# Four small moves in the preparation stage of a four-layer sequence kernel: gate DMAs on ScalarE, modulations in earlier gaps, a QR mask on GpSimd, a division ahead of a QR piece

## The chip, the cores and the metric

The kernel runs on one core of a Trainium2 chip. The metric is the device time of one execution in microseconds (us); of several executions the median is taken. The engines are named as the profile names them: PE is TensorE (matmuls), PEld its weight loads, DVE is VectorE, ACT is ScalarE, POOL is GpSimd, SP is SyncE, which issues most DMAs. A "q" behind a name (SPq, ACTq) is the engine's sequencer, issuing a DMA or taking a branch.

## The reference, cut to what matters

The input `x` is 32 sequences of 128 tokens and 144 channels; `cond` is one vector of 144 per sequence. Four layers follow each other:

- L0: a transformer block. A modulation vector of 6 x 144 per sequence comes from `swish(cond) @ w_mod + b_mod`: a shift and a scale for attention and MLP each, and two gates. Layernorm, modulate, attention with 16 heads of 9 (queries and keys layernormed), gated residual; layernorm, modulate, MLP with GELU, gated residual.
- L1: `U = qr(P).Q` of a 144 x 64 matrix; a 64 x 64 skew matrix per sequence is built from `cond`, `R = expm(A)`; then `x + (z R - z) U^T` with `z = x U`.
- L2: a block like L0 without the norm of queries and keys, with modulations of its own.
- L3: attention as in L2 and a mixture of four experts (two per token), with modulations of its own.

```
mod = swish(c) @ w_mod + b_mod            # once for L0, L2 and L3
U, _ = jnp.linalg.qr(P);  R = expm(A(cond))
x_rot = x + einsum('btd,nd->btn', z @ R - z, U)
```

## The kernel before, in words

All of `x` stays in SBUF. The kernel walks through **ticks**, from -6 to the end; in each tick one sequence of a layer is at each station of a software pipeline. The station "scores" works on the sequence of this tick (`s0`, its row maxima) and of the tick before (`s1`, its exponentials), "weigh", "sums", "divide" and "project_out" on that of two ticks before (`s2`). Layer 0's 32 sequences start at ticks 0 to 31, layer 1's (L2) at tick 39 (`first`, L1163). Nothing reorders the program: each engine executes its instructions in the order in which the Python code emits them. That order is written by hand: in a tick (L1289 to L1325) the named gaps "a", "e", "t", "stats", "b0", "b", "den", "pre1", "c", "y1", "y2", "d", "z" stand between the stations, and `put` (L1168) hangs other work into (tick, gap).

Beside layer 0 two preparations run, both Python generators of which a gap executes one piece.

- `prep_qr` (L313) makes the Householder QR of `P`, 64 columns, three pieces each. The first broadcasts column j by two PE matmuls (L324), takes two sums of squares on ACT (`n2` L334, `ss` L337) and a copy (L336), and a root on POOL (`nrm`, L335). The second is on DVE: a dot product (L340, waits for ACT), the signed root (L345, waits for POOL), three small steps (L349 to L351), and the mask `m` (L352, from `ss`). The third, on DVE too, makes the weight `w` (L354, L355, which uses `m`) and updates the matrix (L356), which the next column's L324 needs. `prepare_qr` (L1129) places one column in each tick before 0, and two in each tick from 0 to 28: pieces one to three in gaps "a" and "t", and then "den", "y1" and "y2".
- `prep_expm` (L420) first makes the modulations and gates of L2 and L3 (`modulations(1)`, `modulations(2)`, each with `layer_gates`), then the skew matrices from eight loaded parts W4 (four loaded at the start, four issued behind the first use, L448), then the matrix exponentials. `prepare_expm` (L1152) executes one piece at (-2, "z"), and from tick 0 on one at "b" and one at "z".

`layer_gates` (L280) makes the two gate vectors of a layer on PE, copies them to one SBUF buffer `gsb` on ACT (L291; the buffer has one copy, so the next call's copy waits for the DMAs out of it), and SP sends them to DRAM in two DMAs (L293), from where they are later broadcast. The weights of the last modulation (L134, into `mlps`) are loaded in `first_gates` at (-4, "b"), issued by SP behind the gate DMAs.

DMA completion is counted on eight semaphores that all queues share in turn; the issuing engine waits until the previous DMA on the same semaphore has landed.

At the end of a tick of layer 0, `divide_T` (L901, PE) spreads the reciprocal sums into PSUM, gap "y1" follows (a second QR piece on DVE), then `divide` (L906, DVE, multiplies the weighted values into `oT`), gap "y2" (a third QR piece), "d", and after "z" `project_out` (L927, PE), which reads `oT`; `residual` (L916) follows on DVE and L913 on POOL.

Of the kernel before, what the change touches and what calls it, by code (L numbers as in the profile page):

```python
# [12 lines left out]
ALU = mybir.AluOpType  # L13
# [40 lines left out]
TINY = 1e-18  # L54
# [11 lines left out]
def tile_kernel(ctx: ExitStack, tc: tile.TileContext, a: dict, out: bass.AP):  # L66
    nc = tc.nc
# [212 lines left out]
    def layer_gates(n):  # L280
        w = w_mods[n]
        psg = bank([B, 2, C], f"ps_gate{n}")
        for c in range(2):
            for k in range(2):
                rows = slice(0, KH + k)
                nc.tensor.matmul(
                    psg[:, c, :], csT[rows, k, :], w[k][rows, MODC + c * C : MODC + (c + 1) * C],
                    start=k == 0, stop=k == 1,
                )
        gsb = pp.tile([B, 2 * C], F32, tag="gsb", name=f"gsb{n}")  # L290
        nc.scalar.copy(gsb, psg.rearrange("b n c -> b (n c)"))  # L291
        for c in range(2):
            nc.sync.dma_start(  # L293
                gates[n, c].rearrange("(b c) -> b c", c=C), gsb[:, c * C : (c + 1) * C]
            )

# [16 lines left out]
    def prep_qr():  # L313


        u0 = pq.tile([128, D], F32, name="u0")
        ssa = pq.tile([128, D], F32, name="ssa")
        rca = pq.tile([128, D], F32, name="rca")
        tau = pq.tile([128, D], F32, name="tau")
        tri = cst[:, K_TRI : K_TRI + D]  # L320
        for j in range(D):
            n = C - j
            ps = bank([128, n + 1], f"ps_qr{j}")
            nc.tensor.matmul(  # L324
                ps, ident[:, j : j + 1].to_broadcast([128, 128]), at[:, j:], start=True, stop=True
            )
            row = small.tile([128, C + 1], F32, tag="qrr", name=f"qrr{j}", bufs=2)
            s = small.tile([128, 8], F32, tag="qr", name=f"qr{j}")
            d, al, n2, nrm, m, den, w = (s[:, i : i + 1] for i in range(7))
            ss, rec, uj = (t[:, j : j + 1] for t in (ssa, rca, u0))  # L330
            junk = small.tile([128, C], F32, tag="qrj", name=f"qrj{j}", bufs=2)
            junk2 = small.tile([128, C + 1], F32, tag="qrk", name=f"qrk{j}", bufs=1)

            nc.scalar.activation(junk2[:, : n + 1], ps, AF.Square, accum_out=n2)  # L334
            nc.gpsimd.tensor_tensor(nrm, n2, half, ALU.pow)  # L335
            nc.scalar.copy(row[:, : n + 1], ps)  # L336
            nc.scalar.activation(junk2[:, :n], ps[:, 1:], AF.Square, accum_out=ss)  # L337
            yield

            nc.vector.scalar_tensor_tensor(  # L340
                junk[:, : n - 1], at[:, j + 1 : C], 1.0, row[:, 1:n], ALU.mult, ALU.mult,
                accum_out=d,
            )

            nc.vector.scalar_tensor_tensor(  # L345
                al.bitcast(U32), row[:, 0:1].bitcast(U32), 0x80000000, nrm.bitcast(U32),
                ALU.bitwise_and, ALU.bitwise_or,
            )
            nc.vector.tensor_tensor(uj, row[:, 0:1], al, ALU.add)  # L349
            nc.vector.tensor_tensor(den, uj, al, ALU.mult)  # L350
            nc.vector.reciprocal(rec, den)  # L351
            nc.vector.tensor_scalar(m, ss, 4 * TINY * TINY, tri[:, j : j + 1], ALU.is_gt, ALU.mult)  # L352
            yield
            nc.vector.tensor_scalar(w, at[:, j : j + 1], uj, d, ALU.mult, ALU.add)  # L354
            nc.vector.tensor_scalar(w, w, rec, m, ALU.mult, ALU.mult)  # L355
            nc.vector.scalar_tensor_tensor(  # L356
                at[:, j + 1 : C], row[:, 1:n], w, at[:, j + 1 : C], ALU.mult, ALU.add
            )
            yield
        nc.vector.scalar_tensor_tensor(tau, ssa, 4 * TINY * TINY, rca, ALU.is_gt, ALU.mult)  # L360

        idd = ident[:D, :D]
        v = pq.tile([D, C], F32, name="v")
        nc.vector.tensor_tensor(v, at[:D, :C], cst[:D, K_SU : K_SU + C], ALU.mult)
        dg = pq.tile([D, 2, D], F32, name="dg")
        nc.vector.tensor_tensor(dg[:, 0, :], u0[:D], idd, ALU.mult)
        nc.vector.tensor_tensor(dg[:, 1, :], tau[:D], idd, ALU.mult)
        nc.vector.tensor_tensor(v[:, :D], v[:, :D], dg[:, 0, :], ALU.add)
        tc_ = pq.tile([D, 1], F32, name="tauc")
        nc.vector.tensor_reduce(tc_, dg[:, 1, :], AX.X, ALU.add)  # L370
        yield
        ps = bank([KH, 2, D], "ps_vt")
        for k in range(2):
            nc.tensor.transpose(ps[:, k, :], v[:, k * KH : (k + 1) * KH], idd)
        vt = pq.tile([KH, 2, D], F32, name="vt")
        nc.scalar.copy(vt, ps)
        yield
        ps = bank([D, D], "ps_vv")
        for k in range(2):
            nc.tensor.matmul(ps, vt[:, k, :], vt[:, k, :], start=k == 0, stop=k == 1)  # L380
        ml = pq.tile([D, 6, D], F32, name="ml")
        nc.vector.tensor_scalar(ml[:, 0, :], ps, tc_, None, ALU.mult)
        lev = cst[:D, K_LEV : K_LEV + 6 * D].rearrange("p (l c) -> p l c", c=D)
        for i in range(5, -1, -1):
            nc.vector.tensor_tensor(ml[:, i, :], ml[:, 0, :], lev[:, i, :], ALU.mult)
        xs = pq.tile([D, 2, D], F32, name="xs")
        nc.vector.tensor_copy(xs[:, 0, :], idd)
        nc.vector.tensor_copy(xs[:, 1, :], idd)
        yield
        yt = pq.tile([D, D], F32, name="yt")  # L390
        for i in range(6):
            ps = bank([D, D], f"ps_yt{i}")
            nc.tensor.matmul(ps, ml[:, i, :], xs[:, 1, :], start=True, stop=True)
            nc.vector.tensor_copy(yt, ps)
            yield
            ps = bank([D, 2, D], f"ps_z{i}")
            nc.tensor.matmul(ps[:, 0, :], yt, xs[:, 0, :], start=True, stop=True)
            nc.tensor.matmul(ps[:, 1, :], xs[:, 0, :], yt, start=True, stop=True)
            nc.vector.tensor_tensor(xs, xs, ps, ALU.subtract)
            yield  # L400
        ps = bank([D, C], "ps_y")
        nc.tensor.matmul(ps, xs[:, 0, :], v, start=True, stop=True)
        y = pq.tile([D, C], F32, name="y")
        nc.vector.tensor_scalar(y, ps, tc_, None, ALU.mult)
        yield
        ps = bank([128, C], "ps_uT")
        for h in range(2):
            nc.tensor.matmul(ps[h * D : (h + 1) * D], v[:, :D], y, start=True, stop=True)
        nc.vector.tensor_tensor(uT, cst[:, K_I2 : K_I2 + C], ps, ALU.subtract)
        ur = pq.tile([D, 128], F32, name="ur")  # L410
        nc.vector.memset(ur, 0.0)
        nc.vector.tensor_copy(ur[:, :CR], uT[:D, CM:])
        yield
        ps = bank([128, 2, D], "ps_u")
        nc.tensor.transpose(ps[:, 0, :], uT[:D, :CM], idd)
        nc.tensor.transpose(ps[:, 1, :], ur, idd)
        nc.vector.tensor_copy(uM, ps[:, 0, :])
        nc.vector.tensor_copy(uR, ps[:, 1, :])
# [484 lines left out]
    def divide(s):  # L903
        po = st[s]["ot"][:, : 2 * T].rearrange("p (t q) -> p t q", t=2)
        oT = work.tile([128, 2, T], F32, tag="oT", name=f"oT_{s}")
        nc.vector.tensor_tensor(oT, st[s].pop("on"), po, ALU.mult)  # L906
        st[s]["oT"] = oT
# [243 lines left out]

    def prepare_expm(tick, gap):  # L1152
        nonlocal prep_expm
        if prep_expm and (tick >= 0 and gap in ("b", "z") or (tick, gap) == (-2, "z")):
            said = next(prep_expm, 0)
            if said == 0:
                prep_expm = None
            elif said is not None:
                rot_T.append(said)
# [108 lines left out]
    def fill(tick, gap):  # L1268
        prepare_qr(tick, gap)
        while (tick, gap) == (last_prep, "d") and late is None:  # L1270
            prepare_qr(tick, gap)
            prepare_expm(tick, gap)

        if gap == ("t" if tick < 0 else "den" if tick < first[1] else "stats") and tick in stats:
            ln_stats(stats.pop(tick))
        for f, args in gaps.pop((tick, gap), ()):
            f(*args)
        prepare_expm(tick, gap)

    last_prep = first[1] - 8  # L1280
    for tick in range(-6, first[2] + B + 14):
# [24 lines left out]
        joined = tick >= first[1]  # L1306
        if s2 is not None:
            divide_T(s2)
        fill(tick, "y1")
        if s2 is not None and not joined:  # L1310
            divide(s2)
        fill(tick, "y2")
        if not joined:
            fill(tick, "d")
# [178 lines left out]
```

## Time and profile before

| what | value |
|---|---|
| median of 3 runs | 1423.7 us (1420.84 to 1427.12) |
| the profiled execution | 1412.95 us |
| its span (first to last instruction) | 1411.1 us |
| PE busy | 1333.3 us, 94% |
| DVE busy | 798.3 us, 57% |
| ACT busy | 819.2 us, 58% |
| POOL busy | 623.4 us, 44% |
| `ps_qr` matmul of tick -1, 0, 1, 3, 18, 24 starts at | 30.87, 39.44, 51.42, 73.25, 256.37, 346.45 us |

All times of the profile are counted from the start of the span. A tick is found in the PE timeline by its first L324 matmul (gap "a"); layer 0 fills about the first 460 us. In a row of a timeline the columns are start, length, engine, line, operation, output<-inputs, shape, and in brackets the idle time before it with what ended it. In a table of stretches each engine has its busy time and its number of instructions, and PEclk is the share of TensorE's full clock that was granted. The line numbers are those of the kernel before.

### The profile page before, as it was taken

The page shows a single profiled execution, that of the slowest core. Times are in us where ns is not written, and L with a number is a line of the kernel's source. Part 1 is how long each engine was busy: PE and PEld are TensorE (multiplying, and loading weights), DVE is VectorE, ACT ScalarE, POOL GpSimd, SP SyncE. Part 2 cuts the span into 40 slices and gives each one's busy share as a digit, 9 for nine tenths or more (in the row PEclk, how much of TensorE's full clock was granted, in tenths as well). Part 3 has the DMA queues.
Part 4 walks back from the last instruction along what each step waited for, and adds up shares of the span by engine and source line. Part 5 has one row for each costly group of instructions (what it writes and reads, how often), then busy time and mean ns, then how long its engine had stood idle before and what let it go on. Part 6 is the DMA issues. An engine that isn't in the chain of part 4 may idle for free.

```text
span 1411.1 us, 36544 instructions
## 1 busy us (share of the span) xinstructions
PE 1333.3 (94%) x14530; PEld 976.5 (69%) x14530; DVE 798.3 (57%) x2652; ACT 819.2 (58%) x1912; POOL 623.4 (44%) x1647
## 2 busy tenths in 40 slices
PE   6989898999989988999999999999999999999998
PEld 4667576686766566677767666777776767677765
DVE  5798888877864256565555555544444444343211
ACT  3657767656756445666666666555555555554431
POOL 5567667654643433343333334425252525151522
PEclk9999999999999999999999999999999999999999
DMA  8200000000003100000100000200000000000000
GB/s 221 57 2 19 19 19 2 19 3 20 19 1 117 34 2 18 10 19 10 42 27 18 10 18 11 73 10 18 9 19 9 19 10 18 10 18 2 18 9 9
DMA packets 21612, 34.78 MB, mean 25 GB/s; under 512 B 2176, under 2 KB 12256, under 8 KB 21184
## 3 DMA queue, kind: packets, MB, share of 16 engines
q1 hardware_dynamic: 20848, 31.82, 7.7%
q8 instruction: 117, 1.92, 0.6%
q10 hardware_dynamic: 592, 0.59, 0.2%
q14 instruction: 55, 0.45, 0.1%
HBM read 29.93 MB, written 2.47 MB: 23 GB/s over the span
## 4 chain that ended last, share of the span: by engine, by line
PE 68%; DVE 4%; ACT 2%; issue 1%; POOL 1%; POOLq 0%; DVEq 0%
PE ps_h L673 17%; PE ps_f L953 16%; PE ps_s L849 6%; PE ps_w L849 6%; PE ps_qk L673 5%; PE ps_o L876 5%; PE ps_pj L927 3%; PE ps_v L673 2%; PE ps_o L889 1%; DVE nm L854 1%; PE ps_o L901 1%; PE ps_g L673 1%; DVE oT L906 1%; PE ps_z L985 1%; PE ps_o L808 0%
## 5 line engine op out<-in xcount | busy, mean ns | idle before, releaser
L861 ACT ACTIVATE pr<-ps_w 128x512 f32<-128x512 f32 x384 | 208.5, 596 | 165.4 <-PE ps_w L849 164.7
L854 DVE TENSOR_REDUCE nm<-ps_s 128x4 f32<-128x512 f32 x384 | 246.8, 684 | 82.3 <-PE ps_w L849 68.9
L849 PE MATMUL ps_w<-q,kT 32*128 32x128 f32 x3072 | 236.4, 284 | 0.9 <-ACT hR_m L663 0.6
L849 PE MATMUL ps_s<-kT,qT 32*128 32x256 f32 x1536 | 234.8, 408 | 0.1
L849 PEld LDWEIGHTS ps_w<-q,kT 32*128 32x128 f32 x3072 | 198.6, 187 | 16.1 <-issue 3.6
L947 ACT ACTIVATE hid<-ps_h 128x512 f32<-128x512 f32 (+1 forms) x224 | 119.2, 590 | 119.1 <-PE ps_h L673 119.1
L953 PE MATMUL ps_f<-mlps,hid 128*128 128x144 f32 x1280 | 181.2, 292 | 0.5 <-ACT hid L947 0.5
L953 PEld LDWEIGHTS ps_f<-mlps,hid 128*128 128x128 f32 x1280 | 165.1, 191 | 18.4 <-issue 11.6
L913 POOL TENSOR_TENSOR x_sb<-x_sb,res_a 128x144 f32<-128x144 f32 x96 | 47.0, 489 | 266.8 <-DVE res_a L916 266.7
L1064 DVE SCALAR_TENSOR_TENSOR acc<-ps_f,cw,acc 128x144 f32<-128x144 f32 x128 | 46.9, 367 | 197.6 <-PE ps_f L953 175.8
L849 PEld LDWEIGHTS ps_s<-kT,qT 32*128 32x128 f32 x1536 | 135.0, 186 | 26.8 <-issue 9.2
L673 PE MATMUL ps_h<-hM_m,mlps 128*128 128x512 f32 x304 | 143.8, 606 | 0.0
L876 PE MATMUL ps_o<-pr,vaug 128*32 128x128 f32 x3072 | 104.8, 277 | 0.4 <-issue 0.4
L876 PEld LDWEIGHTS ps_o<-pr,vaug 128*32 128x32 f32 x3072 | 78.7, 110 | 33.8 <-PE ps_w L849 19.0
L673 PEld LDWEIGHTS ps_h<-hM_m,mlps 128*128 128x128 f32 x304 | 53.4, 190 | 66.2 <-issue 64.7
L906 DVE TENSOR_TENSOR oT<-on,ps_o 128x256 f32<-128x256 f32 x96 | 40.0, 417 | 96.3 <-PE ps_o L808 92.9
L953 PEld LDWEIGHTS ps_f<-pair,hid 128*128 128x128 f32 x640 | 82.3, 190 | 9.6 <-issue 8.4
L953 PE MATMUL ps_f<-pair,hid 128*128 128x144 f32 x640 | 86.8, 287 | 0.2 <-ACT hid L947 0.2
L913 POOL TENSOR_TENSOR x_sb<-x_sb,res_m 128x144 f32<-128x144 f32 x64 | 32.8, 512 | 111.4 <-DVE res_m L916 111.2
L634 POOL TENSOR_SCALAR rs_m_a<-mv_m_a 128x2 f32<-128x2 f32 x81 | 15.5, 191 | 142.9 <-DVE mv_m_a L632 115.5
L663 ACT ACTIVATE hM_m<-ps_hT_m,modM 128x128 f32<-128x128 f32 x96 | 44.1, 460 | 58.4 <-PE ps_hT_m L661 58.2
L861 ACT ACT_TABLE_LOAD x55 | 70.6, 1283 | 8.4 <-PE ps_w L849 7.6
(312 smaller groups left out, 2823.2 us busy)
## 6 DMA issues: line engine op xcount, KB each, us to landing
gates<-gates SPq DMA_DIRECT2D x48, 288.0 KB, 3.6
x_sb<-in_x SPq DMA_DIRECT2D x8, 288.0 KB, 10.2
out_x<-x_sb SPq DMA_DIRECT2D x8, 288.0 KB, 2.4
mlps<-in_L_mlp SPq DMA_DIRECT2D x2, 1000.0 KB, 6.3
wt<-in_W SPq DMA_DIRECT2D x6, 320.0 KB, 8.0
pair<-in_L_mlp SPq DMA_DIRECT2D x1, 1872.0 KB, 10.1
mlps<-in_L_mlp SPq DMA_DIRECT2D x1, 1872.0 KB, 7.6
mlps<-in_L_wmod SPq DMA_DIRECT2D x4, 290.0 KB, 6.3
```

Source lines behind the costliest of these rows:

```text
L663: nc.scalar.activation(gr[g][f"{k}_{kind}"][:, i, :], ps[:, k == "hR", :], AF.Identity, bias=m[:, sh, b : b + 1], scale=m[:, sc, b : b + 1],)
L673: nc.tensor.matmul(ps, x, y, start=k == 0, stop=k == 1)
L849: nc.tensor.matmul(o, x, y, start=True, stop=True)
L854: nc.vector.tensor_reduce(nmv[:, at0 : at0 + 2, ONE : ONE + 2], view.rearrange("p (r t k) -> p r t k", t=2, k=T), AX.X, ALU.max, negate=True,)
L861: nc.scalar.activation(pr[:, 4 * e : 4 * e + 4, :].rearrange("p s q -> p (s q)"), view, AF.Exp, scale=SCALE,)
L876: nc.tensor.matmul(po[rows4(j), t, :], v[:, 4 * j + 2 * t + r, :], prs[j // 2][:, 4 * (j % 2) + 2 * r + t, :], start=r == 0, stop=r == 1,)
L906: nc.vector.tensor_tensor(oT, st[s].pop("on"), po, ALU.mult)
L913: nc.gpsimd.tensor_tensor(x_sb[:, b, :], x_sb[:, b, :], t, ALU.add)
L927: nc.tensor.matmul(ps, oT[:, t, :], w[:, t, :], start=t == 0, stop=t == 1)
L947: nc.scalar.activation(hid[:n, i], ps[:n], AF.Gelu_apprx_tanh)
L953: nc.tensor.matmul(ps, hid[:, at0, i, :], w2[:, m, :], start=m == 0, stop=m == NFC - 1)
L1064: nc.vector.scalar_tensor_tensor(acc, ps, w, acc, ALU.mult, ALU.add)
```

## The change

The two DMAs of each `layer_gates` are issued by ACT instead of SP. The piece with `modulations(2)` runs at (-1, "b") instead of (0, "b"), so that every later piece of `prep_expm` comes one slot (half a tick) sooner. The mask `m` is computed by POOL in a column's first piece, behind `nrm`, instead of by DVE in the second. In layer 0, `divide` is emitted before gap "y1" instead of after it.

```diff
@@ layer_gates
-            nc.sync.dma_start(
+            nc.scalar.dma_start(
                 gates[n, c].rearrange("(b c) -> b c", c=C), gsb[:, c * C : (c + 1) * C]
             )
@@ prep_qr, first piece
             nc.scalar.activation(junk2[:, :n], ps[:, 1:], AF.Square, accum_out=ss)
+            nc.gpsimd.tensor_scalar(m, ss, 4 * TINY * TINY, tri[:, j : j + 1], ALU.is_gt, ALU.mult)
             yield
@@ prep_qr, second piece
             nc.vector.reciprocal(rec, den)
-            nc.vector.tensor_scalar(m, ss, 4 * TINY * TINY, tri[:, j : j + 1], ALU.is_gt, ALU.mult)
             yield
@@ prepare_expm
-        if prep_expm and (tick >= 0 and gap in ("b", "z") or (tick, gap) == (-2, "z")):
+        if prep_expm and (tick >= 0 and gap in ("b", "z") or (tick, gap) in ((-2, "z"), (-1, "b"))):
@@ the loop over ticks
             divide_T(s2)
-        fill(tick, "y1")
         if s2 is not None and not joined:
             divide(s2)
+        fill(tick, "y1")
         fill(tick, "y2")
```

## The prediction, made before the changed kernel ran

> **What bounds the kernel now.** I read the busy slices of the page first, for where PE is not full, since a PE that is full to the end leaves these edits nothing to win.
>
> ```profile
> PE   6989898999989988999999999999999999999998
> ...
> DVE  5798888877864256565555555544444444343211
> ```
>
> PE is below 9 tenths only in the first third, where the two preparations run beside layer 0, and there DVE stands at 8. The change acts in that part alone. Next the table of stretches, cut at ticks.
>
> ```profile
> 30.87:39.44 8.57, 4.07 (x14) 3.12 (x13) 4.11 (x22) 2.97 (x11) 3.87 (x11) 0.50 0.17 51
> 39.44:51.42 11.98, 11.98 (x144) 8.43 (x143) 8.45 (x36) 5.59 (x22) 6.25 (x20) 0.93 0.02 4
> ...
> 73.25:256.37 183.12, 162.77 (x2115) 126.20 (x2116) 165.18 (x594) 128.21 (x404) 128.26 (x352) 0.98 0.04 12
> ```
>
> The columns are length, busy time of PE, PEld, DVE, ACT and POOL, then the clock. Tick -1 (first row) leaves PE idle for 4.5 of its 8.57 us, at half clock; tick 0 fills PE to the last; ticks 3 to 17 (third row) leave PE 20 us idle in 183. Who ends those waits I took from the list of waits of ticks 3 to 17:
>
> ```profile
> PE ps_qr L324 <- DVE at L356: 6.9, 11, 2.1
> PE ps_o L901 <- DVE rdx L894: 5.7, 7, 1.4
> PE ps_pj L927 <- DVE oT L906: 4.3, 6, 1.0
> ...
> DVE qr L345 <- POOL qr L335: 4.3, 13, 0.4
> DVE qrj L340 <- ACT qrr L336: 1.7, 5, 0.4
> ```
>
> PE waits for DVE; all waits of DVE listed there come to 8.8 us in 183. So **ticks 3 to 17 are DVE's**, ticks -1 and 0 PE's, and ticks 18 to 23 mostly PE's.
>
> **Gate DMAs and modulations (ticks -4 to 1).** They share one stretch and are summed together.
>
> ```profile
> 31.71 0.42 PE L661 MATMUL ps_hT_a<-cst,xr 128*128 128x128 f32 x1
> 36.64 0.87 PE L779 MATMUL ps_qkT<-cst,qkn 128*128 128x128 f32 x3 [4.50 <-DVE qky L750]
> ```
>
> ```profile
> 32.98 0.39 ACT L291 COPY gsb<-ps_gate 32x288 f32<-32x288 f32 x1 [4.68 <-DMA gates<-gsb]
> ```
>
> The first copy into `gsb` ends at 19.52, but SP issues its DMAs only at 24.84, behind five loads of `x_sb`; they land at 32.88, and until then the second copy holds ACT. ACT would issue them at about 19.6: 0.4 to 0.6 us each by the five ACTq issues at the start, inside ACT's idle 1.0 us before 20.56. The second copy then follows its gates at about 31.1 and, behind it, two new issues (1.0 us) stand ahead of the column's L334: at 32.6 instead of 33.28. The queries of L767 come 0.7 us sooner. That would be the whole gain, if PE stayed free.
>
> PE does not stay free, since 80 + 8 matmuls of `modulations(2)` now stand ahead of L779. They need the weights that SP issues at 26.94 and 27.41 and that land at 33.12 and 33.80. SP gets to them about 2 us earlier, but the DMA engines are full until 31 (share 1.1 in every stretch from 20 to 30), with the same bytes ahead of them: I keep 33.8. How long they take is a matter of the clock. At full clock (42.88 to 46.44) it was 3.5 us, at half clock (`modulations(0)`: 11.29 to 15.84, gates 16.96 to 19.09) 6.7 us.
>
> ```profile
> 27.40:30.80 3.40, 3.40 (x89) 3.13 (x87) 2.85 (x15) 0.71 (x2) 0.98 (x3) 1.00 1.10 265
> 30.80:34.20 3.40, 1.33 (x6) 0.86 (x4) 1.97 (x11) 1.22 (x7) 0.69 (x2) 0.50 0.12 28
> ```
>
> The first stretch is `modulations(1)`: PE busy throughout, yet the clock falls to 0.50 right after it and stays there until 41.05. These narrow matmuls do not seem to hold the clock up, so I take half clock: 33.8 + 6.7 = 40.5 for L779 instead of 36.64, **+3.9**; tick 0 loses 3.5 at full clock, **-3.5**; the half clock then lasts a stretch longer, to 44.46, so 3.96 us of other work run at half clock (40.5 to 44.46) instead of 4.41 (36.64 to 41.05), half of the difference, **-0.2**. Sum +0.2. The later W4 loads are used one tick after their issue as now (last landing 9.1 us after the first use ends; PE waited 0.8), with a tick 0 some 2 us shorter against a use at the same gap: I add **+0.3**. Upper bound +2. Lower bound, full clock throughout: 33.8 + 3.5 = 37.3, +0.7 - 3.5, and 4.41 us of half clock saved at half their length, 2.2: -5.0.
>
> The Trainium skill ("TensorE: Matmul & The Clock Gate", What's actually happening) says that about 3.4 us of sustained matmuls release the full clock and an idle window of that length takes it away. By it, filling the gap would keep the clock up and this part would give the -5.0; the stretch of 27.40, busy and followed by 0.50, speaks against it.
>
> The one-slot shift moves no work in or out: what DVE and PE do sooner in each tick they do not do in tick 24. The branch of L594, which stalls PE 2.1 us at 343.8, moves from "z" to "b" of tick 23. Nothing, +-1.5.
>
> **Mask on POOL.** The row of a second column (tick 8) and its neighbours:
>
> ```profile
> 138.87 0.16 DVE L351 RECIPROCAL rca<-qr 128x1 f32<-128x1 f32 x1
> 138.96 0.20 DVE L352 TENSOR_SCALAR qr<-ssa,cst 128x1 f32<-128x1 f32 x1
> 139.07 0.41 DVE L906 TENSOR_TENSOR oT<-on,ps_o 128x256 f32<-128x256 f32 x1
> 139.39 0.27 DVE L354 TENSOR_SCALAR qr<-at,u,qr 128x1 f32<-128x1 f32 x1
> 139.70 0.27 DVE L355 TENSOR_SCALAR qr<-qr,rca 128x1 f32<-128x1 f32 x1
> ```
>
> The group's mean is 195 ns, but from its start to the next one's is 0.11 us: that is what goes. L355 gains a wait on POOL beside its wait on DVE. What a second wait costs is seen at L356: in first columns, where the built program gives it two (DVE and PE), it starts 0.38 us after L355, in second columns with one, 0.31. So 0.111 - 0.075 = 0.036 us a column, over the 34 columns of DVE's ticks (3 to 17, 24, 25): **-1.2**. Bounds: 64 x 0.111 = -7.1 if the wait is free, +1 if POOL's extra 0.28 us each (start of L634 to that of L635) reaches L345. The mask itself is in time: it would end 0.78 us or more ahead of L355 in every column, by the end of `nrm` plus 0.3. L913 and the Newton steps queue behind it, with 1 to 4 us of POOL idle per tick.
>
> The Trainium skill ("VectorE: DVE Perf Modes", The DRAIN you can't avoid) measures semaphores between Vector instructions at no extra cost. By it the step would be -7.1 over all columns; L356's 0.38 against 0.31 differs, and I go by that.
>
> **Division ahead of "y1".** L906 now stands ahead of L340 and waits for L901 on PE. What it should end is PE's wait for `oT`:
>
> ```profile
> 138.30 0.38 PE L901 MATMUL ps_o<-cst,rdx 128*128 128x128 f32 x2
> ...
> 139.53 0.76 PE L927 MATMUL ps_pj<-L_wproj,oT 128*128 128x144 f32 x4 [0.74 <-DVE oT L906]
> 140.62 0.45 PE L324 MATMUL ps_qr<-at,cst 128*128 128x121 f32 x2 [0.34 <-DVE at L356]
> ```
>
> `oT` comes 1 us sooner, but the next thing on PE is L324, and that starts 0.14 us after the end of L356, in 12 of the 15 ticks: the 4.3 us of waits move from L927 to L324. L356 itself is not sooner, as DVE does the same work before it. Where DVE's row maxima end before L901 does, DVE now stands idle with the whole QR column behind it, and L324, ACT and POOL behind that. From the timelines (end of L901 minus end of the second L854): tick 5 107.18 - 106.68, 8 138.68 - 138.18, 10 164.31 - 163.82, 14 215.55 - 215.05, 26 379.87 - 379.37: 0.5 each; tick 13 0.24; the rest of DVE's ticks have 0.2 to 0.7 to spare. **+2.7**. Bounds: -4.3 (all of L927's waits) and +4.5 (0.5 in all nine ticks with a shortfall, 18, 27 and 28 being the others).
>
> **Sum.** +0.2 + 0.3 - 1.2 + 2.7 = **+2.0 us**. The profiled execution took 1412.95 (span 1411.1 and 1.85 around it), 10.75 below the median of the three runs; it becomes 1415.0. On the scale of the median, 1423.7 + 2.0 = **1425.7**.
>
> **Rivals.** *Faster*: the clock stays up in tick -1 (-5.0) and the second wait is free (34 x 0.111 = -3.8), the division costs nothing: -8.8, 1414.9. For it: the clock did rise at 27.39 before; against it, the 0.50 that followed. *Slower*: the division's wait. DVE stalls 0.5 us wherever L901 is later than the maxima; it decides from some 14 ticks on (7.1/0.5). If moving the preparation by half a tick made it so in all 29 ticks of the QR, with 0.6 each including the start: +17, 1441. Against it: in most ticks it is DVE's own L894 that L901 waits for, and then DVE is the late one. *The slot is not free*: the modulations only move from a full to a held-up PE; that is my forecast with the other parts at zero, 1424.
>
> **How the numbers follow.** Forecast (and the free-slot case, which falls inside 0.5%) 0.75, faster rival 0.14, slower rival 0.11. About 0.5%, 7.1 us, is what a measurement of this kernel can tell from no change. The faster rival's lower part and the slower one's upper part lie beyond that, so faster 0.13, same 0.75, slower 0.12. The range takes in -5.0 - 7.1 at the low end (1412) and +2 + 4.5 + 1 with a part of the slower rival above (1434).
>
> **What would show it.** Right: L779 of tick -1 at about 40 with PEclk 0.50 before it; the gate copy no longer waiting for a DMA; L355 0.37 after L354; waits of L906 for L901 of 0.5 us, and L324 waiting for L356 where L927 did. Wrong: full clock in tick -1, L354 to L355 still 0.30, no such waits of L906, or a shorter stretch between ticks 3 and 18 than 183 us by over 3 us.

## The result, and the profile after

| | kernel before | changed kernel |
|---|---|---|
| median (lowest to highest), first set | 1419.5 us (1410.3 to 1427.1), 18 runs | 1422.5 us (1415.1 to 1425.2), 18 runs |
| the same in a later set | 1419.0 us (1410.2 to 1427.4), 35 runs | 1419.8 us (1412.5 to 1422.6), 12 runs |
| profiled execution (span) | 1412.95 us (1411.1) | 1425.14 us (1423.2) |

The ratio of the first set is 1.002, with a 95% interval of 1.0001 to 1.0039: **2.8 us slower**, by the interval 0.1 to 5.5. The later set gives 1.0004 (0.9973 to 1.0035), which is no difference that can be told. The forecast was +2.0. The total came near it, but its terms did not: the modulations were put at about nothing and gain 2 to 3 us, and the mask was put as a gain and costs time. They are taken apart below.

Two things stand ahead of every comparison. All 181 runs of the kernel before lie between 1408.8 and 1428.7 (median 1419.4), so its profiled execution is one of its fastest and the median of three on which the forecast was scaled (1423.7) is a high one. And the profiled execution of the changed kernel is one of its slowest: the 12.2 us between the two traces are mostly not the change.

The busy slices of the changed kernel's page, the two rows shown of before:

```profile
PE   7989798998989999999999999999999999999998
...
DVE  5688888876864246656555555534344444344211
```

The first third looks as before: PE full or nearly, DVE at 8. The rows of the table of stretches, for tick -1, tick 0, ticks 3 to 17 and tick 23 (columns: length, then busy time of PE, PEld, DVE, ACT and POOL, the clock, DMA):

```profile
32.98:43.16 10.18, 10.18 (x101) 8.73 (x101) 2.92 (x16) 3.50 (x12) 3.90 (x11) 1.00 0.04 10
43.16:55.38 12.22, 11.72 (x89) 7.50 (x87) 7.68 (x30) 5.76 (x22) 6.68 (x22) 1.00 0.28 70
76.65:263.56 186.91, 166.66 (x2147) 129.79 (x2148) 158.14 (x564) 128.33 (x404) 138.85 (x383) 0.95 0.04 12
339.53:356.47 16.94, 13.47 (x116) 9.36 (x115) 10.09 (x37) 9.28 (x28) 8.20 (x25) 0.80 0.01 3
```

Tick -1 is now full on PE (4.07 of 8.57 before, 10.18 of 10.18 now). Its clock of 1.00 is not to be believed: the trace's records of the clock begin only at 49 us, and the table prints 1.00 where none exists. Lengths tell it. In the PE timeline of that tick:

```profile
34.03 4.49 PE L269 MATMUL ps_mod<-csT,mlps 72*128 72x32 f32 x78
...
38.52 1.89 PE L286 MATMUL ps_gate<-mlps,csT 72*32 72x144 f32 x7
40.34 1.12 PE L779 MATMUL ps_qkT<-cst,qkn 128*128 128x128 f32 x4
```

The modulations take 6.3 us from 34.03 and L779 starts at 40.34; the prediction had 6.7 and 40.5. The four transposes of L779 take 1.12 us, against 0.66 for the same four in tick 7 at full clock: half clock, as forecast. Ticks 3 to 17 take 186.91 us in this trace. In the second trace of the same kernel (run e14) they take 183.05, against 183.12 before:

```profile
74.11:257.16 183.05, 161.68 (x2146) 126.72 (x2147) 158.10 (x564) 128.42 (x404) 139.32 (x383) 0.98 0.04 12
```

Ticks 5 to 9 are equal in both traces of the changed kernel (11.34, 10.67, 10.67, 11.32, 12.81 us, each within 0.01), so what differs from before there (10.74, 10.39, 10.38, 10.72, 12.11) is the program's. Ticks 3 (14.04 and 12.29) and 10 (15.14 and 12.99) differ between the two traces with the half clock that falls in them (0.95 and 0.98 on the mean): that is the execution's.

What DVE waits for in ticks 3 to 17 of the changed kernel (waited for: us in total, times, longest; its L338 to L353 are one line further down than in the kernel before, so L346 is L345 there, and L338 is the mask):

```profile
DVE qkn L767 <- POOL qky L763: 6.5, 13, 0.6
DVE qr L346 <- POOL qr L335: 4.6, 13, 0.4
...
DVE oT L906 <- PE ps_o L901: 1.5, 3, 0.6
```

The first row did not exist before, and the prediction did not have it. The third is the wait it did have. On PE, in the same ticks:

```profile
PE ps_qr L324 <- DVE at L356: 11.0, 11, 1.3
...
PE ps_pj L927 <- DVE oT L906: 0.8, 2, 0.4
```

Before these were 6.9 and 4.3: the wait moved from L927 to L324 as forecast, 11.2 together before and 11.8 now.

**The new wait, read from one tick.** POOL around the first column of a tick, before (tick 7) and after (tick 6):

```profile
120.52 0.54 POOL L335 TENSOR_TENSOR qr<-qr,half 128x1 f32<-128x1 f32 x1
121.03 0.49 POOL L913 TENSOR_TENSOR x_sb<-x_sb,res_a 128x144 f32<-128x144 f32 x1
121.48 0.25 POOL L760 TENSOR_TENSOR qkh<-qkv,qky 128x32 f32<-128x32 f32 x1
...
123.75 0.25 POOL L763 TENSOR_TENSOR qky<-qky,qkh 128x32 f32<-128x32 f32 x1
```

```profile
114.67 0.55 POOL L335 TENSOR_TENSOR qr<-qr,half 128x1 f32<-128x1 f32 x1 [0.15 <-ACT qrk L334]
115.32 0.31 POOL L338 TENSOR_SCALAR qr<-ssa,cst 128x1 f32<-128x1 f32 x1
115.71 0.49 POOL L913 TENSOR_TENSOR x_sb<-x_sb,res_a 128x144 f32<-128x144 f32 x1
116.16 0.25 POOL L760 TENSOR_TENSOR qkh<-qkv,qky 128x32 f32<-128x32 f32 x1
```

The mask is L338. From the start of the root L335 to that of L913 it was 0.51 us and is 1.04, and L913 and the eight Newton steps L760 to L763 follow back to back: POOL does not stand idle once in this row. The step at its end is what L767 on DVE needs, before and after:

```profile
124.31 0.45 DVE L767 TENSOR_TENSOR qkn<-qkraw,qky 128x288 f32<-128x288 f32 x1
```

```profile
118.75 0.46 DVE L767 TENSOR_TENSOR qkn<-qkraw,qky 128x288 f32<-128x288 f32 x1 [0.55 <-POOL qky L763]
```

Before, L763 had ended 0.31 us ahead of it. Counted over ticks 3 to 17, that margin was 0.30 to 0.32 in eleven ticks and 0.5 to 0.6 in four; now it is 0.03 in 14 of 15.

Last, tick 23: the branch of L594 moved from gap "z" to "b", and holds PE longer.

```profile
PE ps_qr L324 <- PEq L594: 3.5, 1, 3.5
```

Before it was 2.1 us, ahead of L927; the tick grew from 14.91 to 16.94 us.

### The profile page after: what moved, and what is told of

It is laid out like the page before. It is cut to its first block, busy times and chain, and to the rows that moved or that the text cites. A ratio compares the mean times of both kernels' runs of the same rounds, so it can differ in the third digit from the quotient of the medians.

```text
span 1423.2 us, 36616 instructions
## 1 busy us (share of the span) xinstructions
PE 1347.2 (95%) x14530; PEld 988.8 (69%) x14530; DVE 786.7 (55%) x2588; ACT 819.6 (58%) x1912; POOL 645.1 (45%) x1711
## 4 chain that ended last, share of the span: by engine, by line
PE 68%; DVE 3%; POOL 2%; ACT 1%; issue 1%; POOLq 0%; DVEq 0%
PE ps_h L673 18%; PE ps_f L953 15%; PE ps_s L849 6%; PE ps_w L849 6%; PE ps_qk L673 5%; PE ps_o L876 5%; PE ps_pj L927 3%; PE ps_v L673 2%; PE ps_o L889 1%; PE ps_o L901 1%; DVE nm L854 1%; PE ps_g L673 1%; DVE oT L906 1%; PE ps_z L985 1%; PE ps_o L808 0%
## 5 line engine op out<-in xcount | busy, mean ns | idle before, releaser
L849 PE MATMUL ps_s<-kT,qT 32*128 32x256 f32 x1536 | 237.9, 414 | 0.0
L913 POOL TENSOR_TENSOR x_sb<-x_sb,res_a 128x144 f32<-128x144 f32 x96 | 47.0, 489 | 268.7 <-DVE res_a L916 266.7
L876 PEld LDWEIGHTS ps_o<-pr,vaug 128*32 128x32 f32 x3072 | 80.1, 112 | 33.6 <-PE ps_w L849 18.9
L906 DVE TENSOR_TENSOR oT<-on,ps_o 128x256 f32<-128x256 f32 x96 | 40.1, 418 | 100.5 <-PE ps_o L808 92.6
L913 POOL TENSOR_TENSOR x_sb<-x_sb,res_m 128x144 f32<-128x144 f32 x64 | 31.9, 499 | 104.2 <-DVE res_m L916 103.7
```

The costliest lines, as they stand in the source:

```text
L849: nc.tensor.matmul(o, x, y, start=True, stop=True)
L876: nc.tensor.matmul(po[rows4(j), t, :], v[:, 4 * j + 2 * t + r, :], prs[j // 2][:, 4 * (j % 2) + 2 * r + t, :], start=r == 0, stop=r == 1,)
L913: nc.gpsimd.tensor_tensor(x_sb[:, b, :], x_sb[:, b, :], t, ALU.add)
```

## The experiments

Letters: **A** gate DMAs on ScalarE, **B** modulations two at (-1, "b"), **C** mask on GpSimd, **D** division ahead of "y1". The changed kernel is A+B+C+D. Each median is of 12 runs. The runs were taken in five sets, each on one chip and with the kernel before beside them: e1 to e4; e5, e6, e9 and e10; e11 to e14; e15 to e18; e19 and e20 (medians of before: 1419.6, 1419.1, 1419.0, 1419.4, 1419.7). The ratio is to the kernel before in the same set, with its 95% interval; it is not the quotient of the two medians.

| run | edits | median (lowest to highest), us | ratio (interval) |
|---|---|---|---|
| e1_gates | A | 1420.0 (1414.7 to 1426.1) | 1.0005 (0.998 to 1.003) |
| e2_mods | B | 1416.8 (1413.9 to 1419.5) | 0.9983 (0.9962 to 1.0004) |
| e3_mask | C | 1421.8 (1411.0 to 1428.9) | 1.0005 (0.9974 to 1.0036) |
| e4_divide | D | 1420.6 (1415.3 to 1426.5) | 1.0009 (0.9987 to 1.0031) |
| e10_gates_mods | A+B | 1418.0 (1415.7 to 1423.4) | 0.9999 (0.9977 to 1.0022) |
| e5_no_mask | A+B+D | 1420.0 (1417.8 to 1423.1) | 1.0006 (0.9988 to 1.0025) |
| e9_no_divide | A+B+C | 1418.7 (1416.5 to 1422.6) | 0.9999 (0.9975 to 1.0022) |
| e6_mask_second | A+B+D, C for second columns | 1420.0 (1415.8 to 1426.7) | 1.001 (0.9988 to 1.0032) |
| e11_mods_pad | B, later pieces in old slots | 1416.5 (1413.7 to 1420.5) | 0.9979 (0.9953 to 1.0004) |
| e12_wide | 4 wide matmuls in tick -1 | 1418.2 (1410.7 to 1422.0) | 0.9981 (0.9953 to 1.0009) |
| e13_no_gates | B+C+D | 1421.7 (1417.2 to 1425.5) | 1.0015 (0.9984 to 1.0046) |
| e14_after_again | A+B+C+D | 1419.8 (1412.5 to 1422.6) | 1.0004 (0.9973 to 1.0035) |
| e15_mods_mask | B+C | 1421.1 (1416.4 to 1424.7) | 1.0011 (0.9994 to 1.0028) |
| e16_mods_divide | B+D | 1417.4 (1413.0 to 1421.8) | 0.998 (0.9958 to 1.0001) |
| e17_mods_again | B | 1416.9 (1413.3 to 1420.6) | 0.9987 (0.9967 to 1.0006) |
| e18_pad_wide | e11 and 3 wide matmuls | **1412.9** (1411.0 to 1416.1) | **0.9958 (0.9938 to 0.9979)** |
| e19_wide_gates | e18 + A | 1412.8 (1408.7 to 1418.0) | 0.9963 (0.9934 to 0.9991) |
| e20_wide_divide | e18 + D | 1418.0 (1415.9 to 1423.4) | 1.0001 (0.9976 to 1.0025) |

### Each edit by itself (e1 to e4)

Each kernel is the kernel before with the lines of one edit of the diff above.

**e1_gates.** 

> Only the two gate DMAs go to ScalarE; all else as in the kernel before. Theory on record: the second copy into gsb no longer waits for a DMA (4.68 us of ACT wait before), it runs near 31.1 and the queries of tick -1 come 0.7 us sooner into a PE that is free there, so the whole gains 0.7 us; tick 3 starts 0.7 sooner. Rival (the DMA engines are full until 31, or ACT's own issue costs as much as the wait): no change, 0. Neither says anything of ticks 3 to 17, which stay at 183 +- 1 us.

**e2_mods.** 

> Only modulations two come at (-1, b), the later pieces of that preparation half a tick sooner. Theory on record: L779 of tick -1 starts at about 40.5 instead of 36.6, tick 0 gives back 3.5, in all +0.5 us (-5.0 to +2), and tick 23 keeps its length though its branch moves to gap b. Rival (the branch in the middle of tick 23 holds more behind it than at its end): tick 23 takes 16.9 us instead of 14.9, so +2.5 us in all, and ticks 3 to 17 stay at 183 +- 1.5 us.

**e3_mask.** 

> Only the mask is on GpSimd. Theory on record: ticks 3 to 17 get 1.1 us shorter (0.036 a column), no new wait on DVE. Rival, seen in the profile after: on POOL the mask stands ahead of L913 and the eight Newton steps L760 to L763, which end about 0.5 us later behind it, and L767 on DVE, which had 0.3 us to spare, waits 0.5 us for L763 in most ticks; then ticks 3 to 17 get 2 to 5 us longer and the whole 3 to 6 us.

**e4_divide.** 

> Only the division stands ahead of gap y1. Theory on record: L906 waits 0.5 us for L901 in some six ticks, PE's wait moves from L927 to L324, +2.7 us in all (-4.3 to +4.5). Rival, by the profile after, where L906 waits only 1.5 us in three of ticks 3 to 17 and the waits that end at L927 fall from 4.3 to 0.8 us: the two cancel, ticks 3 to 17 take 183 +- 1 us and the whole is unchanged within 1 us.

By time none of the four can be told from the kernel before by itself, whose runs spread over 17 us. B comes nearest, with an interval that ends at 1.0004, and its runs lie closer together: their standard deviation is 1.6 us, that of before 4.8. The traces say more. *A*: tick 3 starts at 77.15, not 0.7 sooner than 73.25 but 3.9 later, because tick 0 takes 18.80 us instead of 11.98. The same happens in e4 (18.94), where nothing ahead of tick 0 was changed, but not in e3 (12.02): so tick 0 of the kernel before seems to have two lengths, and the trace on which I worked showed the short one. *B*: tick -1 takes 12.33 and tick 0 12.14, tick 23 17.13 (the rival's number), ticks 8 and 9 23.8 instead of 22.8. *C*: L767 waits for L763 6.5 us in 13 of the ticks 3 to 17, ticks 6 and 7 take 10.93 and 10.91 us (10.39 and 10.38 before), the stretch 185.69. That is the rival; the runs, 2.2 us above before by the medians (-3.7 to +5.1 by the ratio), do not settle its size. *D*: L906 waits 3.0 us for L901 in ticks 3 to 17, six times, the longest 0.5. Ticks 5, 8, 13, 14 and 26 are each 0.4 to 0.6 us longer, and tick 10 2.0: the six ticks the prediction named, the last with a half clock in it. Of the six waits one (0.54 us) is in tick 4, which it had not named. The stretch takes 188.24 us, not the rival's 183; the runs, 1.0 us above before (-1.8 to +4.4 by the ratio), fit both.

### What the half clock of tick 0 hangs on

The table of stretches, cut at the 3.41 us steps in which the clock's records change. First e1, where tick 0 runs from 37.12 to 55.92 (the column behind POOL is the clock):

```profile
33.10:36.50 3.40, 2.18 (x7) 1.92 (x8) 1.29 (x5) 1.05 (x3) 2.15 (x6) 0.50 0.05 17
36.50:39.90 3.40, 3.40 (x13) 2.03 (x13) 1.02 (x5) 1.57 (x8) 1.08 (x4) 0.50 0.00 0
39.90:43.30 3.40, 3.40 (x16) 3.39 (x16) 3.16 (x12) 1.24 (x4) 1.78 (x7) 0.50 0.00 0
43.30:46.70 3.40, 3.40 (x77) 3.30 (x77) 0.01 (x1) 0.00 (x0) 0.97 (x4) 0.50 0.00 0
46.70:50.20 3.50, 3.50 (x18) 2.38 (x14) 1.02 (x6) 0.64 (x3) 0.00 (x0) 0.50 0.02 5
50.20:53.60 3.40, 3.40 (x13) 2.29 (x12) 2.09 (x9) 1.71 (x8) 2.42 (x6) 0.50 0.02 5
53.60:57.00 3.40, 3.40 (x37) 1.51 (x39) 1.70 (x7) 1.64 (x7) 0.22 (x1) 1.00 0.02 5
```

PE is busy to the last from 36.5 on, and still the clock stays at half for five steps. The 77 matmuls of 43.3 to 46.7 are the narrow ones of modulations two (72x32), which began at 42.24. In the kernel before, the clock rose at 41.05, ahead of them (they began at 42.88), and stayed up. So theory K: **narrow matmuls do not bring the clock up, wide ones do**. It is not the whole of it: the first step of e1 that PE fills (36.5) has no narrow one in it and did not raise the clock either. B takes the narrow ones out of tick 0. Ticks -1 and 0 together take 20.6, 21.3, 26.6 and 26.9 us in the four traces with neither B nor wide matmuls (before, e3, e4, e1), and 19.9 to 24.5 in the twelve with B and no wide ones: the long case is gone. Tick -2, ahead of it, still takes anything from 5.0 to 9.3 us. What is new in e12 and later in e18, written here as one function:

```
+    def wide(n):
+        ps = bank([128, 512], "ps_wide")
+        for _ in range(n):
+            nc.tensor.matmul(ps, ident, cst[:, :512], start=True, stop=True)
+    put(-1, "b", wide, 4)          # e12, on the kernel before
+    put(-2, "a", wide, 1)          # e18, on e11
+    put(-1, "b", wide, 2)          # e18, ahead of modulations two
```

**e12_wide.** 

> The kernel before with four matmuls of 128x512 more at (-1, b), whose result nobody reads: PE is busy with wide matmuls through its wait of tick -1. Theory K (windows of wide matmuls bring the clock up, the narrow ones of the modulations do not count): the clock is full before modulations two run in tick 0, tick 0 takes 12 us and not 18.8, and the whole takes 1413 to 1417 with a spread below 8 us. Rival (the clock's phase is a matter of chance that PE's work does not settle): 1419.5 to 1420, 1411 to 1428 as before.

```profile
31.90:35.30 3.40, 3.40 (x8) 1.85 (x8) 2.96 (x18) 1.91 (x8) 2.30 (x7) 0.51 0.29 69
35.30:38.80 3.50, 3.50 (x14) 2.05 (x13) 0.68 (x4) 0.77 (x3) 1.57 (x5) 0.99 0.16 38
38.80:42.20 3.40, 3.32 (x27) 2.73 (x25) 1.50 (x9) 2.31 (x12) 1.50 (x5) 1.00 0.00 0
42.20:45.60 3.40, 3.40 (x88) 2.93 (x87) 3.23 (x14) 0.96 (x3) 1.69 (x7) 1.00 0.00 0
45.60:49.00 3.40, 3.40 (x15) 2.43 (x15) 1.71 (x5) 1.12 (x7) 2.90 (x9) 0.50 0.04 11
```

One step filled with wide matmuls and the clock is up at 35.3, ahead of modulations two; then a step full of narrow ones (42.2, 88 instructions) and it falls to 0.50, PE at 3.40 of 3.40. Tick 0 takes 14.60 us. The time is in between: 1418.2, over 11.3 us, the slowest run 1422.0 where before has 1427.4. Theory K holds in this trace; its numbers (12 us for tick 0, at most 1417, a spread below 8) did not, since the narrow step took the clock away again.

**e11_mods_pad.** The condition of `prepare_expm` also has `and (tick, gap) != (0, "b")`. 

> Modulations two at (-1, b) and nothing at (0, b), so that all later pieces keep their slots; the rest as before. Theory A (modulations out of tick 0 is the gain, the half-tick shift of the later pieces is a loss of its own): ticks -1 and 0 as in the run with the modulations alone, tick 23 back from 17.1 to 14.9 us and ticks 8 and 9 back from 23.8 to 22.8, so 1414 to 1415 and a narrow spread. Theory on record (the shift moves no work in or out): 1416.8, as the modulations alone.

Ticks 23 (14.88) and 8 and 9 (22.8) came out as theory A says; ticks -1 and 0 took 21.0 us, where e2 had 24.5. The time, 1416.5, is 1.5 us above what it had at most and cannot be told from B alone (1416.8).

**e17_mods_again.** 

> Modulations two ahead alone, once more: 1416.8 with a spread of 6 us if the first set told the program; 1419 if that set was chance.

**e18_pad_wide.** 

> Modulations two at (-1, b), later pieces in their old slots, and three matmuls of 128x512 whose result nobody reads: one ahead of the first L324 of tick -2, where PE waits 1.05 us, two ahead of modulations two, where PE waits 3 us for the weights when the clock is full. Theory K (wide work brings and holds the clock up): the clock is full from about 20 to 23 us on and in tick 0, ticks -2 to 0 take 26 to 27 us together (28.5 to 31.7 in the runs with modulations ahead), and the whole 1413 to 1415. Rival (the clock does not follow the shape of the work, and the three cost 1.2 us each at half clock): 1417 to 1420.

1416.9 and 1412.9. B gains 2.5 us again; its two sets together (24 runs) lie 2.9 us below before on the mean, 1.7 to 4.2 when the recorded runs are resampled, so its gain is hardly chance. e18 is 4.0 us below B on the same chip (the old slots are in this too; against e11, which has them, it is 3.6). Steps of e18:

```profile
21.70:25.10 3.40, 3.40 (x7) 1.62 (x6) 3.09 (x16) 1.18 (x4) 2.07 (x6) 1.00 1.12 291
25.10:28.50 3.40, 3.40 (x49) 3.15 (x51) 2.09 (x12) 2.12 (x9) 2.20 (x6) 1.00 1.12 308
28.50:32.00 3.50, 3.50 (x78) 2.32 (x65) 3.05 (x18) 0.27 (x1) 0.33 (x2) 1.00 0.40 79
32.00:35.40 3.40, 3.34 (x86) 3.08 (x86) 2.96 (x18) 1.50 (x8) 2.73 (x7) 1.00 0.08 16
35.40:38.80 3.40, 3.40 (x14) 2.41 (x12) 0.66 (x5) 1.58 (x4) 1.00 (x5) 0.50 0.05 13
```

(The records begin at 25.1, so the 1.00 of the first row is not one of them.) The clock is up through modulations one, the wait for the weights and most of modulations two; the step full of narrow ones again costs one step of half clock. Ticks -2 to 0 take 25.2 us together, and 24.5 and 22.4 in e19 and e20, which have the same three matmuls; they take 26.2 to 31.7 in the twelve traces with B and no wide ones, and 26.4 to 33.5 in the four with neither. No run put narrow matmuls in the same three places, so that any further work for PE there would do as well is not excluded.

### Mask and division on a quieter base

**e5_no_mask.** 

> The changed kernel with the mask on VectorE again. Theory M (the mask on POOL makes L763 late and holds L767): no wait of L767 for L763, ticks 6 and 7 take 10.4 us (10.67 in the changed kernel), 2.5 us faster than the changed kernel, 1420. Theory on record (the mask gains 1.2): 1.2 us slower than the changed kernel, 1423.7.

**e6_mask_second.**

```
-            nc.gpsimd.tensor_scalar(m, ss, ...)
+            if j >= 6 and j % 2 == 1:
+                nc.gpsimd.tensor_scalar(m, ss, ...)
...
+            if not (j >= 6 and j % 2 == 1):
+                nc.vector.tensor_scalar(m, ss, ...)
```

> The changed kernel, with the mask on POOL only in the second column of a tick (gap den), on VectorE in the others. Only the first column's POOL part (gap a) has L913 and the Newton steps behind it, so theory M gives no wait of L767 for L763, ticks 6 and 7 at 10.4 or a little less, and 1419.5 to 1420. If the mask in gap a is harmless and the second column's costs the time: 1422.5 as the changed kernel.

**e9_no_divide.** 

> The changed kernel with the division behind y1 again. Theory D (L906 ahead of y1 stalls DVE 0.5 us in six ticks, as on record): no wait of L906 for L901, 2.5 us faster than the changed kernel, 1420; ticks 6 and 7 take 10.9 us, as with the mask alone, since the division ahead gave 0.25 of the mask's wait back there. Rival (the division is free, and the whole loss is the mask's): 1422.5.

**e10_gates_mods.** 

> Gate DMAs on ScalarE and modulations two ahead; mask and division as before. The modulations alone gave 1416.8, with runs from 1413.9 to 1419.5 where the kernel before has 1411.5 to 1428.6. Theory A (the filled tick -1 gives each execution the same clock around tick 0, the gate DMAs add nothing): 1416.8 +- 1, a spread of 4 to 7 us, tick -1 and tick 0 together about 24.5 us. Rival (that median was chance, and the two steps are worth the +0.5 on record): about 1420, runs spread as before.

In the traces theory M is plain: no wait of L767 for L763 in e5, e6 and e10, 6.7 us in 14 ticks in e9; ticks 6 and 7 at 10.39 and 10.42 (e5), 10.35 and 10.35 (e6), 10.94 and 10.93 (e9). So only the first column's mask, which has L913 and the Newton steps behind it, brings the wait. By time all four lie within 2 us of each other (1418.0 to 1420.0) and within 1.5 of the numbers expected, and decide nothing between mask and division: on A+B the mask costs 0.7 us (e9) and the division 2.0 (e5). A+B spreads over 7.7 us, a little more than theory A had, and its ticks -1 and 0 took 20.6 us, not about 24.5.

**e15_mods_mask.** 

> Modulations two ahead and the mask on GpSimd. Theory M: L767 waits for L763 6.5 us in ticks 3 to 17, ticks 6 and 7 take 10.9 us, and the whole is 1 to 2.5 us slower than the modulations alone of this call. Theory on record: 1.2 us faster than them.

**e16_mods_divide.** 

> Modulations two ahead and the division ahead of y1. Theory on record: L906 waits 0.5 us for L901 in about six ticks, 2.7 us slower than the modulations alone of this call. Rival (what L906 waits is given back where PE's wait at L927 goes): within 1 us of them.

On one chip with e17: **the mask costs 4.2 us** (1421.1 against 1416.9; 1.8 to 5.4 when the runs are resampled), the division 0.4. Beside the 0.7 on A+B, the sign of the mask's price is the firm part; in the traces it lengthens ticks 3 to 17 by 2.6 us here (185.41 against 182.78 in e17) and by 1.3 there (182.86 against 181.60). The first row of DVE's waits in ticks 3 to 17 of e15, and PE's two rows in e17 (no division ahead) and e16 (division ahead):

```profile
DVE qkn L767 <- POOL qky L763: 6.8, 14, 0.6
```

```profile
PE ps_qr L324 <- DVE at L356: 7.1, 10, 2.1
PE ps_pj L927 <- DVE oT L906: 5.3, 7, 1.0
```

```profile
PE ps_qr L324 <- DVE at L356: 13.7, 11, 1.6
...
PE ps_pj L927 <- DVE oT L906: 1.4, 4, 0.4
```

The stretch takes 182.78 us in e17 and 182.73 in e16: 3.9 us leave L927, 6.6 arrive at L324, L906 waits 2.4 us, and nothing is won or lost.

**e20_wide_divide.** 

> The kernel of e18 with the division ahead of y1. Here the later pieces stand in the slots of the kernel before, for which the step was priced: L906 waits 0.5 us for L901 in ticks 5, 8, 10, 13, 14 and 26. Theory on record: 2.7 us slower, 1415.6. Rival (the waits at L927 that go away pay it back): 1412.9 +- 0.8, with ticks 5 and 8 0.5 us longer and others shorter.

Neither: 1418.0, **5.1 us slower** than e18 and 5.2 slower than e19 (e18 with A), which ran beside it on the same chip. L906 waits as priced in ticks 5, 8, 10, 13, 14 and 26, and for 0.54 us more in tick 4; in ticks 3 to 17:

```profile
DVE oT L906 <- PE ps_o L901: 3.0, 6, 0.5
```

Ticks 5, 8, 10, 13 and 14 take 0.55, 0.56, 0.45, 0.43 and 0.56 more than in e18, 2.55 in all (the prediction had 2.2 for these five). Tick 4 takes 1.95 more, and so it does in e4 (13.74 and 14.05, against 11.88 before and 12.10 in e18): in e20 the half clock lasts three steps, from 78.9 to 89.1, where e18 has two and before one. (In e1, without D, it also lasts three, and tick 4 takes 12.93 us: the longer half clock may be the execution's.) Tick 11 gives back 0.6. The whole stretch is 187.64 against 183.29. So D's price seems to depend on where the pieces of the other preparation stand. In their old slots the stretch takes 188.24 and 187.64 us with D (e4, e20) and 183.0 to 184.3 without (six traces); in the changed kernel's, half a tick earlier, 182.7 to 183.8 with D (e5, e6, e16) and 181.6 to 183.3 without (e2, e10, e17). The times are less clear: 5.2 (e20) and 1.0 (e4) in the old slots, 0.4 (e16) and 2.0 (e5) in the new ones.

### The gate DMAs

**e13_no_gates.** 

> The changed kernel with the gate DMAs on SyncE again. In the changed kernel's trace ACT spends 0.3 to 1.4 us in each of these issues, and two pairs stand ahead of work that PE waits for (L334 and L782). Theory G (the DMAs on ScalarE cost about 1.5 us): 1.5 us faster than the changed kernel of the same call, 1420.5. Theory on record (they gain 0.7): 0.7 slower than it.

**e14_after_again.** 

> The changed kernel itself once more, beside the others of this call and for a second trace: 1422 by its runs so far; tick 5 and 8 with L906 0.5 us behind L901 and ticks 6 and 7 at 10.67 us again if these belong to the program, the half clock in ticks 3 and 10 elsewhere if that belongs to the execution.

**e19_wide_gates.** 

> The kernel of e18 (modulations ahead, slots kept, three wide matmuls) with the gate DMAs on ScalarE, beside its 1412.9. Theory on record for this step: 0.7 us faster, 1412.2. Theory G: two issues of 0.4 us or more ahead of L334 and of L782, with PE full behind them, 1 to 2 us slower, 1414 to 1415. Within 0.7 us of 1412.9: it does neither.

e13 and e14, side by side, say that A gains 1.9 us. Counted from the median of before in each one's own set, A costs 0.5 alone (e1), 1.6 on B (e10 and e2) and 2.9 on B+D (e5 and e16), and gains 2.1 on B+C (e9 and e15) and 0.5 on e18 (e19). There is no common sign: A is worth nothing that these runs can show. The issues on ACT are there to be seen. The second and third pair in the changed kernel:

```profile
33.50 1.71 ACTq L293 DMA_DIRECT2D gates<-gsb  x2
35.31 0.29 ACT L334 ACTIVATE qrk<-ps_qr 128x140 f32<-128x140 f32 x1 [1.84 <-DMA gates<-gsb]
...
40.86 0.78 ACTq L293 DMA_DIRECT2D gates<-gsb  x2
41.69 0.47 ACT L782 ACTIVATE qT<-ps_qkT,g 128x256 f32<-128x256 f32 x1 [0.86 <-PE ps_qkT L779]
```

The first of them holds L334 for 1.8 us, but PE has modulations two to do until 40.3 and does not ask for it.

## Why the prediction was right or wrong

- **Gate DMAs.** Right: issued at 18.91, inside ACT's idle time, 0.8 us for the pair; no copy into `gsb` waits for a DMA any more. Two new issues ahead of L334 were put at 1.0 us and took 1.71, without an effect. No gain, as forecast for a PE that is not free.
- **Modulations two: the step that failed.** "Tick 0 loses 3.5 at full clock", "the half clock then lasts a stretch longer, -0.2", sum +0.2. L779 (40.34) and the half clock in tick -1 were right. Wrong was to take tick 0 of one trace, 11.98 us, as the kernel's: in e1 and e4 it took 18.8 and 18.9. The term measures **-2.8 (e2) and -2.5 (e17)** by the medians; each interval ends just above no change (1.0004 and 1.0006), but both sets together, resampled as above, do not reach it. The runs also lie closer together: a standard deviation of 1.6 and 2.0 us against 4.8 and 4.1 of before beside them. The prediction had the row that tells why: 27.40 to 30.80, PE full of modulations, and 0.50 behind it. I used it to argue that the moved modulations run at half clock, and did not ask what they do to the clock of the tick they leave. The +0.3 for the W4 loads is too small to be seen in the times; PE's weight load waited 0.8 us for them before, 0.5 in the changed kernel and 1.0 in e17.
- **One-slot shift: nothing, +-1.5.** Not refuted as a sum, but "moves no work in or out" hid large parts: tick 23 +2.0, ticks 18 to 22 +0.7, ticks 8 and 9 +1.0, given back in ticks 13 (-1.2) and 24 (-0.5) among others. From tick 3 to tick 28, e2, e10 and e17 take 320.9 to 322.9 us, and e11, e18 and e19, without the shift, 320.2 to 322.2; the runs of e11 against e2 show 0.3 us.
- **Mask: -1.2 was wrong in sign.** On DVE the steps were as worked out: L355 starts 0.36 after L354 (0.37 forecast, 0.30 before). The failed sentence is that L913 and the Newton steps queue behind the mask "with 1 to 4 us of POOL idle per tick". That idle time lies elsewhere in the tick; between L335 and L763 POOL is full, and at the end of that row stood 0.31 us of margin. The mask moves it by 0.53, not by the 0.28 taken from one start to the next: it starts 0.65 us after L335 did, where L913 had started after 0.51, and L913 follows 0.39 later. The term measures **+4.2** on B alone and +0.7 on A+B; beside the division, which gives back 0.25 of 0.54 us in ticks 6 and 7, 2.5 and -0.2 (1422.5 and 1419.8 with it, 1420.0 without).
- **Division: +2.7.** The mechanism, the ticks (but for tick 4), the 0.5 us and the move from L927 to L324 are right. The size is open: 5.2 and 1.0 in the old slots, where 1.95 of the stretch's 4.35 in e20 is tick 4 with its longer half clock, and 0.4 and 2.0 in the new ones. The prediction priced it in the slots of before, which its own other edit moves.
- **The sum.** That +2.0 came near +2.8 and +0.6 is luck: a gain of 2 to 3 that it had at zero met a loss of up to 4 that it had as a gain. On the absolute scale 1425.7 was 3.2 too high, as the three runs of before were. The faster rival named the right place (the clock of ticks -1 and 0) with the wrong mechanism: the clock does not stay up in tick -1; tick 0 is rid of what kept it down.

What stays open: the single terms do not add up (C costs 4.2 on B, 0.7 on A+B and between -0.2 and 2.5 on A+B+D), and it is not known why a step that PE fills without narrow matmuls raises the clock in one place and not in another.

## What to carry to other kernels

Idle time of an engine per tick is no cover for an instruction put into its queue: read the row of instructions behind that place, to the one that another engine waits for, and its margin there. Where a kernel's runs spread over 17 us, one trace is one draw: look for a tick that may have another length before pricing against it. And a part that works with narrow matmuls is better put where PE would wait anyway than in a tick that needs the full clock, which gained 2 to 3 us here; three wide matmuls that nobody reads, in PE's waits ahead of it, gained some 4 us more.

## What the runs showed of the hardware

- **The clock is decided per step of 3.41 us, and PE need not be idle to lose it.** In the twenty traces the recorded clock is 1.0 or 0.5, and each stretch of either lasts a multiple of 3.41 us. Between 57 and 1390 us, 65 of the 66 steps at full clock with PE busy for less than 0.51 of the step were followed by half clock, 46 of 162 between 0.51 and 0.645, and 17 of 7387 above. From e18, tick 3:

```profile
79.80:83.20 3.40, 1.50 (x8) 0.60 (x8) 3.23 (x15) 0.68 (x3) 2.63 (x7) 0.99 0.00 0
83.20:86.60 3.40, 3.10 (x18) 2.70 (x22) 2.84 (x12) 1.24 (x7) 1.08 (x4) 0.50 0.02 5
```

  The Trainium skill ("TensorE: Matmul & The Clock Gate", HAM oscillation — how this bites in real kernels) gives as its abstract rule no idle gaps of PE over about 3.4 us. Here 1.5 us of work in 3.4, with 1.40 us as the longest gap, did not keep the clock. The same page (What's actually happening) has the step run free of the kernel's start; here the first record of the clock lies anywhere from 22.6 to 49.2 us.
- **Narrow matmuls count for little.** In the first 60 us of the twenty traces, 8 of the 9 steps at full clock that the modulations (72x32 and 72x144, L269 and L286) fill for 0.89 or more were followed by half clock (27.4 before; 42.2 in e12), and none of the 16 that they fill for 0.35 to 0.85. At recorded half clock, with PE busy for 0.95 or more, none of the 14 steps that they fill for 0.46 or more raised it (43.3 in e1), and 12 of the 18 without them did.
- **DVE's L345, one element per partition, took 0.44 us in the first column of each of ticks 3 to 17 before (in tick 7 it ended at 121.54 and POOL's L913 at 121.52), and 0.16 in 14 of these 15 ticks with the mask on POOL, when L913 comes later.** The Trainium skill ("SBUF — State Buffer", SBUF: two separate sides) has a port pair for which a DVE op with two SBUF inputs and a GpSimd op that reads SBUF contend, and which one of them holds for its whole instruction. That would explain it; no run here tested it by itself.
